# Sorting the attention's keys with a network of maxima and minima in a four-layer graph kernel

## The chip, the cores and the metric

The kernel runs on one core of one Trainium2 chip. The metric is the device time of one execution in microseconds. The kernel before took 3454.11 us in the median of three runs (3450.97 to 3459.17).

## The reference, cut to what matters

Four layers follow one another, each with a layer norm ahead of it and its result added to x, which has 6250 nodes of 256 values:

1. A graph layer: every one of 106250 edges joins its source's row with an edge attribute of 256 values, goes through a matrix W1 and a relu, and is averaged over its destination node.
2. A mixture of four experts, whose gates come from a graph attention over 131072 other edges.
3. A graph layer with a weight for each edge.
4. A second mixture of experts.

The change concerns the attention of layer 2. Its sum is a softmax over the edges of a destination:

```
e = leaky_relu(a_src[src] + a_dst[dst]);  e_max = segment_max(e, dst)
ee = exp(e - e_max[dst]);  denom = segment_sum(ee, dst)
agg = segment_sum(h[src] * ee / (denom[dst] + 1e-16), dst)
```

Its edges come in no order. Sums over a destination do not depend on the order either, so the kernel is free to sort.

## The kernel before, in words

The engines are TensorE (PE, matmuls), VectorE (DVE), ScalarE (ACT), GpSimd (POOL) and SyncE (SP). All arithmetic of the layers is in fp32. Nodes lie in 49 windows of 128, one node a partition.

The kernel first norms x and multiplies it with one half of W1 (y_dram). In this part `make_keys` builds, for every partition, 1024 keys of the attention's edges: one fp32 bit pattern each, with the destination (counted from the top) in its high bits and the source in its low ones. A larger key is a smaller destination, so that keys sorted downwards are edges sorted by destination.

Then comes the loop of the first graph layer (from L1598), which the change lives in. It has 147 iterations q and two more to drain: three for each window w, with six tiles of 128 edges in each. In iteration q,

- `join(q - 1)` (VectorE, L1485) adds the gathered source rows to the product of the edge attributes, and ScalarE does the relu (L1486);
- `hidden(q, 0)`, `hidden(q, 2)` and `hidden(q, 4)` (TensorE) multiply the transposed attributes `et` with the other half of W1 into `ph`, two tiles at a time;
- `add_up(q - 2)` (TensorE, L1508, L1500 for the last window) sums the rows of each destination, by a matmul with the 0/1 matrix `eq`;
- `load_sources(q + 2)` (GpSimd, L1128) gathers six source rows for each partition, and `load_attr` (SyncE, L1376) loads edge attributes up to four iterations ahead;
- `turn(q + 1)` (VectorE, L1467) transposes the attributes of the next iteration in blocks of 32 x 32 into `et`;
- `equal(q)` (VectorE, L1217) writes `eq`. A window's edges are sorted by destination already, so a tile needs only some quarters of its 128 nodes (`QUARTERS`); the last window takes all four.

Three generators fill the gaps between these: `work` (the end of each window, `end_of`, L1514), `sort` (the attention's sort) and `slow` (`windows`, which finds the edges of later windows, and ends near iteration 80). `steps` lets each of its generators do one step. `end_of`, `windows` and `sorted_edges` share a single PSUM buffer named pt.

The loop's order is fixed: `ordered.pin()` chains the instructions of each engine in the order in which the program gives them. So on VectorE and on TensorE an instruction that waits holds up all that stands behind it. The order in the loop around the change:

```
if 0 < q <= NQ1: join(q - 1)
if q < NQ1: hidden(q, 0)
steps(sort)
... add_up(q - 2); load_sources(q + 2); turn(q + 1); load_attr
if q < NQ1: hidden(q, 2)
steps(*([sort] if q % 2 else []))
... equals[q] = equal(wk, *groups1[q]); hidden(q, 4)
steps(slow)
```

The sort before (`sort_steps`, L1276) takes the eight largest keys of a partition with one instruction (L1279), writes them to `order`, and strikes them out of `key` with another (L1282, two instructions on the engine). 106 rounds give the 848 largest. Each of the two is one step; there is one step in each iteration between `join` and `turn` and, in odd iterations, a second one ahead of `equal`. The sort so takes 212 steps and is done in iteration 141. Then `sorted_edges` (L1285) runs as one piece: it takes the sources and the two halves of the destination out of `order`, turns one of these with five matmuls and sends it to DRAM (`low_dram`), and fills and compares limits with 160 small memsets.

The second part, the experts of layer 2 and their attention, begins when the loop has drained at about 1310 us; layers 3 and 4 follow. The change touches none of these.

Of the kernel before, what the change touches and what calls it, by code (L numbers as in the profile page):

```python
# [8 lines left out]
F32 = mybir.dt.float32  # L9
I32 = mybir.dt.int32  # L10
AF = mybir.ActivationFunctionType
OP = mybir.AluOpType
# [4 lines left out]
P = 128  # L17
# [851 lines left out]
def kernel(ctx: ExitStack, tc: tile.TileContext, a: dict, out: bass.AP):  # L869
# [11 lines left out]
    T = -(-N // P)  # L881
# [10 lines left out]
    C2 = E2 // P  # L892
# [6 lines left out]
    G1 = 6  # L899
    NG = CW // G1  # L900
    NT = G1 // 2
    NR = CW // NT
    Q = P // 4
    QUARTERS = ((0, 1), (0, 2), (1, 3), (1, 4), (2, 4), (3, 4))
# [16 lines left out]
    KA, KB, KT, KM, NK = 640, 544, 848, 596.0, 12  # L921
# [5 lines left out]
    V, SC, TE, GP, SY = nc.vector, nc.scalar, nc.tensor, nc.gpsimd, nc.sync  # L927
# [4 lines left out]
    def near_blocks(g):  # L932

        k = g * G + G / 2
        mid = k * (N / KM) / P
        spread_of = (C2 * (k / C2) * (1 - k / C2)) ** 0.5 * (N / KM) / P
        n = min(NK, int(-(-2 * (4.2 * spread_of + 0.9) // 1)))
        b0 = min(max(round(mid - n / 2), 0), T - 2)
        return b0, min(max(round(mid - n / 2) + n, b0 + 2), T) - b0
# [4 lines left out]
    with ExitStack() as fast:  # L944
# [51 lines left out]
        if T1 > C1:  # L996
            V.memset(flat.bitcast(I32)[:, C1:T1], 2**24)
            n = E1 - C1 * P
# [199 lines left out]
        def quarters(w, k):  # L1198

            return QUARTERS[k] if w < T - 1 else (0, 4)  # L1200

        def chunk(q):


            return [(k, t) for k in (q, q + NG) for t in range(NT)]

        def equal(pool, w, q):


            eq = pool.tile([P, G1 * P], F32, name="eq", bufs=3)  # L1210
            found, at = {}, 0
            for k in (q, q + NG):
                lo, hi = quarters(w, k)
                n = (hi - lo) * Q
                found[k] = eq[:, at : at + NT * n].rearrange("p (t n) -> p t n", n=n)
                at += NT * n
                V.tensor_tensor(  # L1217
                    found[k], lane[:, None, lo * Q : hi * Q].to_broadcast([P, NT, n]),
                    dst1[:, w, k, :].unsqueeze(2).to_broadcast([P, NT, n]), op=OP.is_equal,
                )  # L1220
            return found
# [51 lines left out]
            )  # L1273
            V.tensor_tensor(key.bitcast(I32)[:, half], raw[0], raw[1], op=OP.bitwise_or)

        def sort_steps(k):  # L1276

            top = order[:, k * 8 : (k + 1) * 8]
            V.max(out=top, in_=key)  # L1279
            yield  # L1280
            if k * 8 + 8 < KT:
                V.match_replace(out=key, in_to_replace=top, in_values=key, imm_value=0.0)  # L1282
            yield

        def sorted_edges(pst, wk):  # L1285

            k = order.bitcast(I32)
            V.tensor_scalar(src2, k[:, 0:KA], 8191, None, op0=OP.bitwise_and)
            some = key[:, 0:KT]
            for v, s in ((high, 20), (low, 13)):  # L1290
                vi = some.bitcast(I32)
                V.tensor_scalar(
                    vi, k, s, 127, op0=OP.logical_shift_right, op1=OP.bitwise_and
                )
                V.tensor_copy(some, vi)
                V.tensor_scalar(some, some, -1.0, 127.0, op0=OP.mult, op1=OP.add)
                V.tensor_copy(v, some)
            for c in range(KA // P):
                pt = pst.tile([P, 4, P], F32, name="pt")
                TE.transpose(pt[:, 0, :], some[:, c * P : (c + 1) * P], ident)  # L1300
                lt = wk.tile([P, P], BF16, name="lt")
                SC.activation(lt, pt[:, 0, :], AF.Copy)
                SC.dma_start(low_dram[c * P : (c + 1) * P, :], lt)
            V.tensor_add(good2[:, 1:2], good3[:, 0, 0:1], good3[:, 1, 0:1])
            V.tensor_add(good2[:, 3:4], good3[:, 0, 1:2], good3[:, 1, 1:2])

            lim = key[:, 0:KA]
            for g in range(KA // G):
                V.memset(lim[:, g * G : (g + 1) * G], float(near_blocks(g)[0]))
            hit = order[:, 0:KA]  # L1310
            V.tensor_tensor(hit, high[:, 0:KA], lim, op=OP.is_ge)
            for g in range(KA // G):
                V.memset(lim[:, g * G : (g + 1) * G], sum(near_blocks(g)) - 0.5)
            V.tensor_tensor(lim, lim, high[:, 0:KA], op=OP.is_ge)
            V.tensor_mul(hit, hit, lim)
            V.tensor_reduce(good2[:, 0:1], hit, axis=AX.X, op=OP.add)
# [5 lines left out]
        with ExitStack() as layer:  # L1322
            layer.enter_context(counting)
            srt = layer.enter_context(tc.tile_pool(name="srt", bufs=1))
            key = srt.tile([P, C2], F32, name="key")
            order = srt.tile([P, KT], F32, name="order")
            wp = layer.enter_context(tc.tile_pool(name="w1", bufs=1))
            wix = layer.enter_context(tc.tile_pool(name="wix", bufs=1))
            wea = layer.enter_context(tc.tile_pool(name="ea1", bufs=3, side="right"))
# [55 lines left out]
            with (  # L1385
# [12 lines left out]
                for t0, t1 in parts0:  # L1398
                    b = t0 // TB
# [5 lines left out]
                    for i in range(t1 - t0):  # L1405
                        t = t0 + i
# [29 lines left out]
            with (  # L1436
# [21 lines left out]
                def load_sources(q):  # L1458

                    w, g = groups1[q]  # L1460
                    for j, (k, t) in enumerate(chunk(g)):
                        gather(rows_of(q)[:, j, 0:D], y_dram, src1[:, w, k, t : t + 1])
# [9 lines left out]
                def hidden(q, j):  # L1472
                    if j == 0:
                        ph[q] = psh.tile([P, G1, D], F32, name="ph")
                    for i in range(j, j + 2):
                        mm(
                            ph[q][:, i, :],
                            lambda c: et[q][:, c, i * 4 : (i + 1) * 4, :].rearrange("p m k -> p (m k)"),
                            lambda c: w1b[:, c, :],
                        )  # L1480

                def join(q):

                    h = rows_of(q)[:, :, 0:D]
                    V.tensor_add(h, ph.pop(q), h)  # L1485
                    SC.activation(h, h, AF.Relu)  # L1486
                    et.pop(q)
# [79 lines left out]
                def windows():  # L1567

                    for b in range(1, NB):
                        for w in range(b * TB, (b + 1) * TB):  # L1570
                            count_below(w)
                            yield
                        find_starts(psm, b)
                        yield
                        yield from load_windows(b, psm)
                        if b == 1:
                            count_good()
                            yield

                def sorting():  # L1580

                    for k in range(KT // 8):
                        yield from sort_steps(k)
                    sorted_edges(psm, wk)

                work, sort, slow = [], [sorting()], [windows()]

                def steps(*more):
                    for some in (*more, work):
                        for n in list(some):  # L1590
                            if next(n, some) is some:
                                some.remove(n)
# [5 lines left out]
                for q in range(NQ1 + 2):  # L1598
                    if 0 < q <= NQ1:
                        join(q - 1)  # L1600
                    if q < NQ1:
                        hidden(q, 0)
                    steps(sort)
                    if q >= 2:
                        add_up(q - 2)
                        if (q - 2) % NG == NG - 1:
                            work.append(end_of((q - 2) // NG))
                    if 3 <= q + 2 < NQ1:
                        load_sources(q + 2)
                    if q + 1 < NQ1:  # L1610
                        turn(q + 1)
                        for n in range(q + 2, min(q + 5, NQ1)):
                            if n not in ahead:
                                ahead[n] = load_attr(n)
                    if q < NQ1:
                        hidden(q, 2)
                    steps(*([sort] if q % 2 else []))
                    if q < NQ1:
                        equals[q] = equal(wk, *groups1[q])
                        hidden(q, 4)  # L1620
                    steps(slow)
                    ordered.pin()
# [113 lines left out]
        with (  # L1736
# [404 lines left out]
            steps, begun, waiting = [[edge_columns(), False]], [], []  # L2141
# [43 lines left out]
            for k in range(NA + 5):  # L2185
# [4 lines left out]
                now, here, there, before = k - 2, k - 3, k - 4, k - 5  # L2190
# [30 lines left out]
            k = NA + 5  # L2221
# [14 lines left out]
        with (  # L2236
# [297 lines left out]
            k = 0  # L2534
# [21 lines left out]
        with (  # L2556
# [6 lines left out]
            n = wk.tile([P, NB + 7], F32, name="n")  # L2563
# [4 lines left out]
            for i in range(2):  # L2568
                k = NB + 1 + 2 * i
# [6 lines left out]
            some = wk.tile([P, 1], F32, name="some")  # L2576
# [48 lines left out]
```

## Time and profile before

| | us |
|---|---|
| Median of three runs | 3454.11 (3450.97 to 3459.17) |
| The profiled execution, its own time | 3456.93 |
| Its span, from first to last instruction | 3455.0 |
| PE busy in the span | 3184.3 (92%) |
| DVE busy | 2305.0 (67%) |
| POOL busy | 2240.7 (65%) |
| ACT busy | 1132.5 (33%) |
| First step of the sort, last step of the sort | 89.8, 1234.1 |

The profile shows one execution. A group of instructions is named by its line in the kernel, its engine, its operation and the tiles it writes and reads, with how often it ran, its busy time in all and the mean of one. Behind it stands the idle time of the engine just ahead of these instructions, and what ended it. Busy times of TensorE have modelled ends, so a busy TensorE is not one at its peak. What counts is which engine sets the pace in a stage, and what it waits for there.

### The profile page before, as it was taken

What the parts mean: (1) busy time and instruction counts of PE and PEld (TensorE: products, weight loads), DVE (VectorE), ACT (ScalarE), POOL (GpSimd) and SP (SyncE); (2) the same over time, 40 slices, a digit from 0 to 9 for tenths busy, and PEclk for the clock granted to TensorE, in tenths of its full rate; (3) what the DMA queues carried; (4) which work ended last, traced back from release to release, by engine and by line L of the source; (5) the groups of instructions that cost most, each with busy time, mean ns of one, the idle gap of its engine ahead of it and who ended that gap; (6) DMA issues with size and microseconds to landing.
All of it is one profiled execution on the core that took longest, in us unless ns stands there. A gap on an engine that the chain in (4) does not pass through costs nothing.

```text
span 3455.0 us, 56503 instructions
## 1 busy us (share of the span) xinstructions
PE 3184.3 (92%) x18509; PEld 2532.5 (73%) x18509; DVE 2305.0 (67%) x5687; ACT 1132.5 (33%) x2014; POOL 2240.7 (65%) x2364
## 2 busy tenths in 40 slices
PE   7899998999999999999999999995678888989898
PEld 5677776777777768888888888893456666666677
DVE  7788888888887876887576757775334444445464
ACT  4122222222222224344545454662012212112133
POOL 0577776777777754766555556634777777777773
PEclk8999999999999999999999999996567777677797
DMA  5899999999999963434334434443112222222221
GB/s 171 200 202 200 196 189 185 192 204 196 209 201 205 200 161 93 109 84 118 101 100 113 117 100 122 118 85 104 52 53 59 59 60 59 59 59 61 64 63 37
DMA packets 699194, 428.51 MB, mean 124 GB/s; under 512 B 531304, under 2 KB 640347, under 8 KB 698892
## 3 DMA queue, kind: packets, MB, share of 16 engines
q1 hardware_dynamic: 601436, 245.05, 30.0%
q0 software_dynamic: 89408, 178.08, 23.0%
q8 instruction: 150, 2.46, 0.3%
q10 hardware_dynamic: 8048, 1.68, 0.2%
q14 instruction: 152, 1.25, 0.1%
HBM read 382.05 MB, written 42.49 MB: 123 GB/s over the span
## 4 chain that ended last, share of the span: by engine, by line
PE 45%; DMA 14%; POOL 13%; DVE 12%; issue 9%; SPq 5%; ACT 2%; DVEq 0%; ACTq 0%; POOLq 0%
PE ph L1115 19%; POOL hg L1128 12%; PE py L1115 11%; PE po L1850 5%; DMA hg<-hp_dram,src 5%; DMA ea<-in_edge_attr_dram 5%; SPq L1376 4%; DVE et L1467 3%; PE pe L2490 2%; PE pt L1115 2%; DVE h L1485 2%; PE pe L1508 2%; DMA rb<-low_dram 2%; DVE order L1279 1%; PE pa L1787 1%
## 5 line engine op out<-in xcount | busy, mean ns | idle before, releaser
L1128 POOL DMA_INDIRECT h<-y_dram,src x882 | 837.0, 949 | 450.5 <-issue 331.8
L1128 POOL DMA_INDIRECT hg<-hp_dram,src x831 | 786.5, 946 | 268.0 <-issue 224.6
L1115 PE MATMUL ph<-w1b,et 128*128 128x256 f32 x3528 | 840.7, 388 | 21.1 <-DVE et L1467 19.7
L1128 POOL DMA_INDIRECT sg<-gat_dram,src x640 | 612.2, 957 | 355.9 <-issue 161.0
L1115 PEld LDWEIGHTS ph<-w1b,et 128*128 128x128 f32 x3528 | 656.1, 192 | 170.9 <-issue 67.7
L2490 PE MATMUL pe<-eq,hg 128*128 128x96 f32 (+15 forms) x2036 | 436.3, 352 | 151.4 <-DMA hg<-hp_dram,src 123.6
L2490 PEld LDWEIGHTS pe<-eq,hg 128*128 128x128 f32 x2036 | 384.7, 258 | 256.2 <-issue 96.7
L2469 DVE TENSOR_SCALAR eq<-px,dst,ew 128x96 f32<-128x96 f32 x831 | 261.9, 369 | 218.7 <-PE pe L2490 135.1
L1115 PE MATMUL py<-w,hh 128*128 128x256 f32 x1568 | 385.6, 386 | 6.0 <-ACT hh L1686 5.4
L1115 PE MATMUL ph<-b_all,w 128*128 128x256 f32 (+1 forms) x1600 | 385.8, 380 | 1.3 <-issue 1.2
L1486 ACT ACTIVATE h<-h 128x1536 f32<-128x1536 f32 x147 | 218.2, 1485 | 399.5 <-DVE h L1485 348.8
L1115 PEld LDWEIGHTS py<-w,hh 128*128 128x128 f32 x1568 | 290.0, 191 | 42.7 <-ACT hh L1686 8.0
L1115 PEld LDWEIGHTS ph<-b_all,w 128*128 128x128 f32 x1600 | 289.9, 190 | 33.8 <-issue 1.6
L1485 DVE TENSOR_TENSOR h<-ph,h 128x1536 f32<-128x1536 f32 x147 | 258.0, 1755 | 42.0 <-PE ph L1115 24.4
L1467 DVE STREAM_TRANSPOSE et<-ea 128x1536 f32<-128x1536 f32 x147 | 259.9, 1768 | 12.3 <-DMA ea<-in_edge_attr_dram 8.0
L1686 ACT ACTIVATE hh<-ph,b 128x256 f32<-128x256 f32 (+1 forms) x400 | 166.6, 467 | 282.0 <-PE ph L1115 277.1
L1850 PE MATMUL po<-pp,B 128*128 128x240 f32 (+10 forms) x1280 | 252.2, 337 | 3.0 <-DVE acc L1856 2.9
L1850 PEld LDWEIGHTS po<-pp,B 128*128 128x128 f32 x1280 | 215.6, 190 | 15.3 <-DVE acc L1856 3.8
L1508 PE MATMUL pe<-h,eq 128*32 128x257 f32 x3168 | 216.8, 384 | 0.0
L1508 PEld LDWEIGHTS pe<-h,eq 128*32 128x32 f32 x3168 | 96.0, 109 | 91.8 <-issue 33.8
L1829 DVE TENSOR_TENSOR pp<-px,A 128x960 f32<-128x960 f32 (+10 forms) x160 | 156.0, 975 | 3.9 <-PE po L1850 3.6
L1110 ACT ACTIVATE b_all<-pt 128x256 f32<-128x256 f32 x147 | 55.0, 383 | 275.3 <-PE pt L1109 274.8
(338 smaller groups left out, 4026.6 us busy)
## 6 DMA issues: line engine op xcount, KB each, us to landing
ea<-in_edge_attr_dram SPq DMA_DIRECT2D x1176, 96.0 KB
y<-y SPq DMA_DIRECT2D x196, 128.0 KB
w<-in_L_ffn_W_dram SPq DMA_DIRECT2D x48, 512.0 KB
y<-ys SPq DMA_DIRECT2D x96, 256.0 KB
rb<-low_dram SPq DMA_DIRECT2D x80, 256.0 KB
h<-y_dram,src POOLq DMA_INDIRECT x882
hg<-hp_dram,src POOLq DMA_INDIRECT x831
sg<-gat_dram,src POOLq DMA_INDIRECT x640
```

The lines of the kernel that those rows point to most:

```text
L1115: TE.matmul(dst, lhs(c), rhs(c), start=c == 0, stop=c == n - 1)
L1128: GP.indirect_dma_start(out=dst, out_offset=None, in_=table[0:NP, :], in_offset=IndirectOffsetOnAxis(ap=idx, axis=0),)
L1376: SY.dma_start(ea[c * Q : (c + 1) * Q, i, :, :], part[:, 2 * c * Q : 2 * (c + 1) * Q].rearrange("(m p) d -> p m d", p=Q),)
L1467: V.transpose(et[q].rearrange("p c m k -> p m c k"), ahead.pop(q).rearrange("p i m (c k) -> p (i m) c k", c=2),)
L1485: V.tensor_add(h, ph.pop(q), h)
L1486: SC.activation(h, h, AF.Relu)
L1508: TE.matmul(sums[w][b * Q : (b + 1) * Q, :], eq[k][:, j, at], h[:, i * NT + j, 0:WS], start=g == 0 and j == NT - 1, stop=g == last_of[b] a ...
L1686: SC.activation(hidden[u][:, f, :n, :], ph[:, f - f0, :n, :], AF.Gelu, bias=b1[:, e, f : f + 1],)
L1829: V.tensor_tensor(pps[g, half][:, :, 0:n, :], pay[:, js, :].unsqueeze(2).to_broadcast([P, HG, n, HV]), near[g][:, js, 0:n].unsqueeze(3).to ...
L1850: TE.matmul(po.rearrange("p b v -> p (b v)"), B[:, j, :], pp[:, j, 0:n, :].rearrange("p b v -> p (b v)"), start=half == 0 and j == 0, stop ...
L2469: V.tensor_scalar(equals[k][:, j, :], lanes[:, 0:NW], dst_of[:, t : t + 1], ew[:, t : t + 1], op0=OP.is_equal, op1=OP.mult,)
L2490: TE.matmul(sums[b][:, lo - t0 * P : hi - t0 * P], hg[:, j, :], eq[:, j, lo - n0 : hi - n0], start=False, stop=after >= (t0 + n) * P,)
```

## The change

The sort becomes a bitonic network. It goes through the sizes 2, 4, ... 1024, and in each size through the steps size/2, ... 1. In each of the 55 passes every key is compared with the one `step` away, the larger goes to one place and the smaller to the other, by one instruction for the maxima and one for the minima, from one of two buffers into the other. Up to size 512 neighbouring runs are sorted in opposite directions, so that a pass has two such pairs of instructions with 256 elements each; in the last size it has one pair with 512. A pair is one step of the generator. After 55 passes, an odd number, the keys lie in `order`.

Both buffers hold 1024 keys now, so `order` grows from 848 to 1024. `equal` gives room: its tile has the size that the largest iteration of an ordinary window needs, half of what it had, and the last window has a tile of its own, `eq4`, with one buffer. The second slot for a step of the sort, in odd iterations, is gone.

```diff
+        EQ = NT * Q * max(
+            sum(QUARTERS[k][1] - QUARTERS[k][0] for k in (q, q + NG)) for q in range(NG)
+        )
+
         def equal(pool, w, q):
-            eq = pool.tile([P, G1 * P], F32, name="eq", bufs=3)
+            total = NT * Q * sum(hi - lo for lo, hi in (quarters(w, q), quarters(w, q + NG)))
+            if w < T - 1:
+                eq = pool.tile([P, EQ], F32, name="eq", bufs=3)
+            else:
+                eq = pool.tile([P, total], F32, name="eq4", bufs=1)
...
-        def sort_steps(k):
-
-            top = order[:, k * 8 : (k + 1) * 8]
-            V.max(out=top, in_=key)
-            yield
-            if k * 8 + 8 < KT:
-                V.match_replace(out=key, in_to_replace=top, in_values=key, imm_value=0.0)
-            yield
+        def sort_steps():
+
+            here, there = key, order
+            size = 2
+            while size <= C2:
+                step = size // 2
+                while step:
+                    a, b = (
+                        v.rearrange("p (n m t s) -> p n m t s", m=size // (2 * step), t=2, s=step)
+                        for v in (here, there)
+                    )
+                    runs = [(slice(0, None, 2), 0), (slice(1, None, 2), 1)]
+                    for some, up in runs if size < C2 else [(slice(0, 1), 0)]:
+                        x, y = a[:, some, :, 0, :], a[:, some, :, 1, :]
+                        V.tensor_tensor(b[:, some, :, up, :], x, y, op=OP.max)
+                        V.tensor_tensor(b[:, some, :, 1 - up, :], x, y, op=OP.min)
+                        yield
+                    here, there = there, here
+                    step //= 2
+                size *= 2
+            assert here is order
 
         def sorted_edges(pst, wk):
-            k = order.bitcast(I32)
+            k = order.bitcast(I32)[:, 0:KT]
...
-            order = srt.tile([P, KT], F32, name="order")
+            order = srt.tile([P, C2], F32, name="order")
...
                 def sorting():
-                    for k in range(KT // 8):
-                        yield from sort_steps(k)
+                    yield from sort_steps()
                     sorted_edges(psm, wk)
...
-                    steps(*([sort] if q % 2 else []))
+                    steps()
```

## The prediction

> **What bounds the kernel now.** I read the page first, then the granted clock (0.90 on the one core), the groups by shape, the windows by stage, the waits, and the timeline around single waits. The sort lies wholly in the first graph layer, the loop from 117 to about 1310 us. Busy times in it:
>
> ```profile
> core 0: us, PE busy (x) PEld busy (x) DVE busy (x) ACT busy (x) POOL busy (x), PEclk, DMA share, GB/s
> 130.00:800.00 670.00, 642.05 (x4229) 490.69 (x4228) 575.62 (x941) 180.73 (x294) 473.11 (x500) 0.99 0.95 197
> 800.00:1225.00 425.00, 419.60 (x2776) 322.06 (x2775) 343.55 (x503) 120.94 (x199) 307.44 (x325) 1.00 1.03 202
> ```
>
> TensorE (PE) is busy for 95.8% of the first stretch and 98.7% of the second, VectorE (DVE) for 86% and 81%. So TensorE sets this stage, and only its idle time, 28.0 + 5.4 us, is there to be won: whatever leaves VectorE. What is the idle time waiting for? The waits from 120 to 800 us (engine and line, released by, total us, times, longest):
>
> ```profile
> PE ph L1115 <- DVE et L1467: 9.4, 21, 2.5
> PE pt L1109 <- DVE ix_g L1164: 8.3, 1, 8.3
> PE pt L1109 <- DVE dst L1170: 4.5, 3, 2.3
> PE pt L1109 <- DVE start L1036: 3.0, 2, 2.1
> PE pt L1115 <- DVE ix_g L1164: 2.1, 3, 0.7
> ```
>
> Nearly all is "VectorE came late": with the transposed edge attributes (et), or with emptying the one PSUM tile pt that the windows' small matmuls and end_of share. From 800 on only et is left (5.1 us, 18 times, in the waits from 800 to 1220). How a late et comes about, in every third iteration, the timeline shows (start, length, instruction, idle before):
>
> ```profile
> 911.17 0.42 DVE L1532 TENSOR_TENSOR o<-pt,b 128x256 f32<-128x256 f32 x1 [3.78 <-PE pt L1115]
> ...
> 913.05 1.76 DVE L1485 TENSOR_TENSOR h<-ph,h 128x1536 f32<-128x1536 f32 x1
> ...
> 914.72 1.22 DVE L1279 MAX8 order<-key 128x8 f32<-128x1024 f32 x1
> ...
> 916.41 1.78 DVE L1467 STREAM_TRANSPOSE et<-ea 128x1536 f32<-128x1536 f32 x1 [0.21 <-issue]
> ...
> 918.33 0.89 PE L1115 MATMUL ph<-w1b,et 128*128 128x256 f32 x3 [0.23 <-DVE et L1467]
> ```
>
> VectorE had been idle for 3.78 us, so it starts this chain on time; the sort's step sits between join (L1485) and turn (L1467), and TensorE waits 0.23 us at the end. The durations:
>
> ```profile
> L1279 DVE MAX8 order<-key 128x8 f32<-128x1024 f32 x106 | 127.9, 1207 | 0.0
> L1282 DVE MATCH_REPLACE8 key<-order,key 128x1024 f32<-128x1024 f32 x105 | 126.8, 1208 | 0.0
> L1282 DVE MATCH_VALUE_LOAD key<-order,key 128x8 f32 x105 | 7.5, 71 | 0.0
> L1532 DVE TENSOR_TENSOR o<-pt,b 128x256 f32<-128x256 f32 x49 | 20.8, 424 | 126.3 <-PE pt L1115 126.3
> L1263 DVE TENSOR_TENSOR last<-last,ix_g 128x512 f32<-128x512 f32 x2 | 1.4, 688 | 0.0
> L1264 DVE TENSOR_REDUCE good<-last 128x1 f32<-128x512 f32 x2 | 1.4, 676 | 0.0
> L1809 DVE TENSOR_REDUCE z<-za 128x32 f32<-128x384 f32 x37 | 31.2, 843 | 0.3
> ```
>
> [...] L1809 reads fp32 at a step of 16 bytes: against L1264, 384 elements take 1.7 cycles each in place of one[...]. [...] The gathers that overlap L1217[...] last 954 ns in the mean against 946 for the rest: next to nothing.
>
> **The change, part by part.**
>
> *Removed:* 127.9 + 126.8 + 7.5 = 262.2 us of VectorE.
>
> *Added:* the sizes 2 to 512 make 45 passes with four instructions of 256 elements, the last ten passes two of 512: [...] Net 172 us less, 5% of the span, but not on TensorE. The step is unknown in the trace for two strided SBUF inputs. Lower bound one cycle per element (L1888 reads runs of four fp32 at that pace: 196 elements in 356 ns); upper bound 1.7 from L1809. [...] I take one cycle; at 1.7 throughout a pair is 1.22 us.
>
> *In an iteration:* the first slot (between join and turn) held one step of 1.21 to 1.29 us; it gets a pair, 2 x 0.424 + gap = 0.88 us: 0.35 us earlier. In q = 90 to 99 the pair is 1.4 us, 0.15 later. The second slot, every odd iteration, between turn and equal, is emptied: 1.25 us earlier for equal, the windows' step and the next join. The network has 100 yields against 212, so it ends at q = 100 and not at 141; the 46 iterations after have no sort.
>
> *Waits for et:* in the windows 1 to 29, about 21 regular ones of 0.27 go, and some 2 us of the longer: 7.5 us. In q = 90 to 99 nothing is won (-0.6). After q = 100, 14 of 0.29: 4. Together 11 us.
>
> *Waits for pt:* 13 stalls, 19.8 us. What VectorE is nearer to the evacuation: 1.6 us in odd iterations, 0.35 in even. The stall of 8.3 us follows a wait of 9.6 us for a transfer (raw_src) and loses 1.6 at most. About half the stalls are each kind: 7 us.
>
> *sorted_edges moves* from q = 141 behind turn to q = 100 ahead of turn. It is 15.8 us of VectorE (L1288 at 1247.1 to L1316 at 1262.9), and TensorE, in order, waits 5.7 us for the first of its five transposes and then for each copy. Behind it stand add_up and the rest of the iteration on TensorE, turn and join on VectorE. Before, the two windows from there took 59.1 us join to join against 2 x 23.55: 12 us lost. In the new place TensorE has hidden(q,0) out of the way, resumes after some 9.7 us, has add_up and hidden(q,2), (q,4) to do (5.2 us), and turn(q+1) lands 17.8 us after the block's start: 12 to 15 us. I count 0, the end is 3 worse. Its five stores go out on the Activation queue as before.
>
> *eq and eq4:* the smaller eq costs nothing in time. eq4 has one buffer: equal(145) waits for add_up(144) (1296.25 at its end, where equal(145) ran at 1287.9), and join(145) behind it comes at 1297.4 in place of 1291.7; add_up(145) at 1301.3 is still met. equal(146) then ends at 1305.2, join(146) at 1307 in place of 1303.4, and add_up(146) is 2.5 to 3.5 us later. The first expert layer's matmuls can fill that; where they don't, 3.5 us. I take 2.
>
> *GpSimd, DMA:* a window of three iterations issues 18 gathers at 1.25 us = 22.5 us against TensorE's 23.3 with its idle taken out; slices of 220 GB/s and more stand beside the mean of 202. Both still cover, with little to spare.
>
> Sum: 11 + 7 - 0 - 2 = 16 us. The profiled execution took 3456.9 us (span 3455.0 and 1.9 around it): 3441. It lies 2.8 above the median of the runs, 3454.1, which becomes 3438. The stages after it run on TensorE too (busy 199 of 200 us from 1400), so the gain is kept.
>
> **Rivals.**
>
> *Nothing to measure.* The gaps close, and something with as little slack takes their place: gathers at 22.5 of 23.3, or edge attributes. For: shares of DMA near 1. Against: both are off the chain at present, gathers being issued 15 us before their join. 3454 less 0 to 6: 3451.
>
> *Much faster.* The ends of matmuls are modelled, so "busy" can hide waits for VectorE. For: its busy 81 to 86%. Against: its idle time shows it waiting for TensorE 58 us at L1532 from 800 to 1225. With a hidden 0.3 us in each of 147 iterations: -44, 3410.
>
> *Slower: strided operands.* If an element of the network's passes costs more than the 1.7 cycles of L1809, the first slot grows and et comes later in each of the 33 windows under the sort. The gains outside that slot are some 7 us net (4 after q = 100, 5 at pt, less 2); they are eaten at 0.21 us more per window, a pair of 1.46 us, 2.15 cycles per element. At 3 cycles a pair is 1.9 us, 33 x 0.66 = 22 lost, net +15: 3469. [...]
>
> **How the numbers follow.** My forecast (8 to 28 us faster) 0.60; much faster 0.10; nothing 0.16; slower 0.14, of it 0.03 for sorted_edges and the last window at their dear ends. A measurement of this kernel can tell about 0.2% (7 us) from no change. The range leaves out half of much faster and most of slower: 3421 to 3457. The forecast alone: 3426 to 3446. Faster 0.70, same 0.16, slower 0.14.
>
> **What would show it.** [...] the waits of PE for et from 130 to 1225 down from 16 us to under 5; waits at pt roughly halved; sorted_edges near 930 us in place of 1247, with a stall of 10 us; equal of the last window waiting for PE pe L1500. The prediction is wrong if the pairs take over 1.4 us, if TensorE's idle time moves to gathers or ea, or if the loop's period falls well below 23.3 us a window.

## The result, and the profile after

The changed kernel took 3430.09 us in the median of six runs (3423.36 to 3434.85) beside 3455.03 us of the kernel before: a ratio of 0.9927, 95% interval 0.9914 to 0.9941, so 25 us or 0.7% faster. The forecast was 3438. The profiled execution of after took 3423.36 us (span 3421.6), the fastest of its six, so a difference of the two profiles (33.4 us of span) is some 8 us larger than one of medians.

Busy times of the loop's two stretches in the kernel after (columns as in the windows of before):

```profile
core 0: us, PE busy (x) PEld busy (x) DVE busy (x) ACT busy (x) POOL busy (x), PEclk, DMA share, GB/s
130.00:800.00 670.00, 658.36 (x4377) 507.70 (x4376) 509.82 (x953) 184.28 (x307) 497.16 (x519) 1.00 1.01 204
800.00:1215.00 415.00, 407.18 (x2690) 313.63 (x2689) 266.98 (x564) 114.49 (x198) 300.39 (x315) 0.99 1.00 201
```

In the first stretch TensorE's idle time went from 28.0 to 11.6 us; in the second it is 7.8 us, 6.6 of them in the one window with `sorted_edges`. VectorE's share fell from 86 to 76% and from 81 to 64%. What TensorE still waits for from 120 to 800 us:

```profile
PE pt L1109 <- DVE ix_g L1164: 3.4, 1, 3.4
PE pt L1115 <- DVE ix_g L1164: 2.1, 3, 0.7
...
PE pt L1109 <- DVE dst L1170: 1.8, 3, 0.6
...
PE ph L1115 <- DVE et L1489: 0.8, 1, 0.8
```

The wait for et is down from 21 times, 9.4 us, to a single one, and those for pt are about half (10.7 us in all against 19.8). In the third iteration of a window, where before the late et cost a visible 0.23 us, the timeline of after reads:

```profile
1009.65 0.42 DVE L1554 TENSOR_TENSOR o<-pt,b 128x256 f32<-128x256 f32 x1 [4.98 <-PE pt L1115]
...
1011.52 1.76 DVE L1507 TENSOR_TENSOR h<-ph,h 128x1536 f32<-128x1536 f32 x1
...
1013.76 1.78 DVE L1489 STREAM_TRANSPOSE et<-ea 128x1536 f32<-128x1536 f32 x1 [0.21 <-DMA ea<-in_edge_attr_dram]
...
1016.20 0.38 PE L1109 MATMUL pt<-ident,o 128*128 128x128 f32 x2
...
1016.41 1.89 PE L1115 MATMUL ph<-w1b,et 128*128 128x256 f32 x8
```

VectorE is idle longer ahead of the chain (4.98 us against 3.78), no sort step stands between join (L1507) and turn (L1489), et is ready at 1015.5, and TensorE passes from the transposes to `ph` with no wait shown.

The groups by shape of the network, and of the last window's `eq4`:

```profile
L1300 DVE TENSOR_TENSOR order<-key 128x256 f32<-128x256 f32 x46 | 19.9, 433 | 0.0
...
L1300 DVE TENSOR_TENSOR key<-order 128x512 f32<-128x512 f32 x5 | 3.4, 689 | 0.0
...
L1225 DVE TENSOR_TENSOR eq<-lane,dst 128x384 f32<-128x384 f32 x6 | 3.0, 547 | 14.7 <-PE pe L1522 14.7
```

All eight groups of maxima and minima lie at 418 to 433 ns for 256 elements and at 682 to 689 for 512; they sum to 90.1 us, as forecast.

Where the time went, by the joins of the two profiles (us). Window w lies between join(3w) and join(3w + 3); the time between them is called its period below.

| stretch | before | after | difference |
|---|---|---|---|
| start to the first join | 117.3 | 114.2 | -3.1 |
| window 0 | 21.6 | 20.8 | -0.7 |
| windows 1 to 29 | 709.1 | 684.4 | -24.7 |
| windows 30 to 47 | 436.2 | 427.4 | -8.8 |
| last window: joins 144 to 146 | 19.1 | 24.0 | +4.9 |
| join 146 to the end of the span | 2151.6 | 2150.7 | -0.9 |

Nearly all of the change acts in three of these rows: 24.7 + 8.8 - 4.9 = 28.6 us. The rest of the kernel keeps what was won; between two profiles of the same changed kernel this rest varied by more than the 0.9 us in the table (2150.7 and 2157.1 from join 146 on).

### The profile page after: what moved, and what is told of

Read it like the earlier page. It is cut to its first block, busy times and chain, and to the rows that moved or that the text cites. A ratio compares the mean times of both kernels' runs of the same rounds, so it can differ in the third digit from the quotient of the medians.

```text
span 3421.6 us, 56392 instructions
## 1 busy us (share of the span) xinstructions
PE 3172.9 (93%) x18509; PEld 2532.1 (74%) x18509; DVE 2137.7 (62%) x5571; ACT 1123.3 (33%) x2014; POOL 2247.8 (66%) x2364
## 4 chain that ended last, share of the span: by engine, by line
PE 61%; POOL 15%; DMA 9%; issue 8%; DVE 4%; ACT 2%; SPq 1%; DVEq 0%; ACTq 0%; POOLq 0%
PE ph L1115 30%; POOL hg L1128 13%; PE py L1115 11%; PE po L1871 6%; PE pe L1530 5%; DMA hg<-hp_dram,src 5%; PE pt L1115 4%; PE pe L2511 2%; POOL h L1128 1%; PE pa L1808 1%; SPq L1398 1%; DMA rb<-low_dram 1%; PE pt L1109 1%; DMA ea<-in_edge_attr_dram 1%; DMA h<-y_dram,src 1%
## 5 line engine op out<-in xcount | busy, mean ns | idle before, releaser
L1507 DVE TENSOR_TENSOR h<-ph,h 128x1536 f32<-128x1536 f32 x147 | 258.2, 1757 | 101.3 <-PE ph L1115 73.8
L1489 DVE STREAM_TRANSPOSE et<-ea 128x1536 f32<-128x1536 f32 x147 | 260.5, 1773 | 12.0 <-DMA ea<-in_edge_attr_dram 8.1
```

Source lines behind the costliest of these rows:

```text
L1489: V.transpose(et[q].rearrange("p c m k -> p m c k"), ahead.pop(q).rearrange("p i m (c k) -> p (i m) c k", c=2),)
```

## Experiments

Two theories stood against each other at first. *Place:* what counts is when turn comes after join, so the sort step between them is to blame, and the rest of the gain is pt coming free earlier. *Load:* VectorE simply had 172 us too much, wherever that stood. Later ones ask what is left. Kernels that ran in different groups ran on different chips (before: 3454.98 in the first, 3462.19 in the second, 3457.02 in the third), so only ratios are compared across groups. "Loop" below is the time from join(3) to join(144) in the profile: 1145.5 us before, 1111.9 after, 1113.8 in a second profile of after.

**Only the place (b_moved).** The kernel before with its old sort, the same instructions on VectorE, but no step between join and turn:

```diff
                         hidden(q, 0)
-                    steps(sort)
+                    steps()
...
-                    steps(*([sort] if q % 2 else []))
+                    steps(*([sort, sort] if q % 2 else [sort]))
```

> The kernel before, with its old sort, but each iteration's step of the sort stands behind turn instead of between join and turn; odd iterations take their two steps there. VectorE's work is the same to the instruction. Theory A (it is the place: what stands between join and turn makes et late, and a wait of 0.27 us costs about 0.47 us a window): the waits of PE for et from 130 to 1225 fall from 16 us to under 4, the windows' period without the windows' own work falls from 23.55 to about 23.1 us, and the kernel takes 3440 us (3432 to 3446); stalls at pt do not get shorter. Rival B (it is the sum of VectorE's work, 172 us less): the same time as before, 3450 to 3459.

Measured: 3436.09 us, ratio 0.995 (0.9936 to 0.9964). Its loop takes 1121.0 us, 24.5 less than before, with not one instruction taken off VectorE. Its waits of TensorE from 120 to 800 us:

```profile
PE pt L1109 <- DVE ix_g L1164: 5.5, 1, 5.5
PE pt L1109 <- DVE dst L1170: 4.6, 3, 2.4
PE pt L1109 <- DVE start L1036: 3.2, 2, 2.2
PE ph L1115 <- DVE et L1467: 2.7, 3, 1.4
```

The waits for et fall from 21 to 3, while those for pt stay nearly as they were (18.1 us in all, against 19.8). So the place does most of it: 24.5 of the 33.6 us that the change takes off the loop. That the rest comes from the emptied second slot is tested below (a_slot2).

**The first slot filled again (a_slot1).** The changed kernel with idle maxima between join and turn, which bring the slot back to about the old step's length (`pad` is a new tile of 8 values; its line is left out here):

```diff
                         hidden(q, 0)
+                    if q < 90:
+                        V.max(out=pad, in_=flat[:, 0:200])
+                    elif 100 < q <= 141:
+                        V.max(out=pad, in_=flat)
+                        V.max(out=pad, in_=lane)
                     steps(sort)
```

> The kernel after, with idle maxima between join and turn that bring this slot back to about 1.25 us in iterations 0 to 89 and 101 to 141 (200 elements beside a pair of the network, 831 and 128 elements where there is no pair). The second slot stays empty. A: the waits for et come back, 44 windows at 0.47 us: 20 us on the 3430 of after, 3450 (3443 to 3455), and the period after iteration 101 is 23.5 us again. B: 84 of the 172 us of VectorE's work are back, so half of the gain: 3442, and the period in between.

Measured: 3446.24 us, 0.9975 (0.9967 to 0.9983); loop 1130.8, 18.9 more than after. The mean period of windows 35 to 46 is 23.69 us instead of 23.05 (23.65 in most of them), and the waits of TensorE from 930 to 1215 us hold one line:

```profile
PE ph L1115 <- DVE et L1490: 5.1, 12, 0.7
```

Twelve waits, 0.43 us in the mean as shown (0.36 in most); 0.64 us a window as the loop pays it. In windows 1 to 29 the same kernel loses 8.9 us, some 0.3 a window, though from 120 to 800 us the view shows a single wait for et. Window 27, for one, takes 23.39 us against 23.06 in after, with 0.10 us of idle time on TensorE. So a late et costs time that the view does not show; how much, is worked out below.

**The second slot filled again (a_slot2).** In odd iterations behind turn, up to q = 141, for the step that the change took away there:

```diff
                         hidden(q, 2)
+                    if q % 2 and q <= 141:
+                        V.max(out=pad, in_=flat)
+                        V.max(out=pad, in_=lane)
                     steps()
```

> The kernel after, with idle maxima of 1.27 us behind turn in odd iterations up to 141, where the old sort had its second step; the slot between join and turn stays short. A: only the stalls at the shared PSUM tile pt come back, which lie before iteration 80: 7 to 11 us, 3439 (3435 to 3444), and the period after iteration 101 stays at 23.05 us. B: 90 of 172 us are back: 3443, spread evenly, with a longer period after iteration 101 too.

Measured: 3435.74 us, 0.995 (0.9936 to 0.9963); loop 1119.5, 7.6 more than after. The period after iteration 101 stays at 23.05. Most of what it costs lies in windows 1 to 29 (6.1 us), where TensorE's idle time goes from 11.1 to 18.1 us. Of these 7.0 us, 4.8 are shown at pt and 2.4 at ph, behind VectorE's work on a window's end (rc).

**Both (a_both).**

> The kernel after with both slots filled as in the two kernels above: VectorE's timetable is that of before, the network and the place of sorted_edges are new. A: 3430 + 20 + 9 = 3459 (3453 to 3464), that is before plus the 4.8 us by which the last window with one eq4 buffer is later. If moving sorted_edges were part of the gain, it would stay: 3445 or less.

Measured: 3454.79 us, 1.0001 (0.9993 to 1.0009); loop 1143.3. With VectorE's two slots at their old length the whole gain is gone, although the sort is a network and `sorted_edges` still stands at iteration 100. The two halves add up: 0.0048 + 0.0023 of the ratio alone, 0.0074 together (in the loops of the profiles 18.9 + 7.6 us alone, 31.4 together, 5 us more). Moving `sorted_edges` is worth nothing that can be seen: in its new place its window takes 35.78 us, 12.1 more than the mean of its neighbours (23.65), and in the old place it cost 12.0.

**No sort at all (a_nosort).** One copy takes the network's place:

```diff
-                    yield from sort_steps()
+                    V.tensor_copy(order, key)
+                    for _ in range(100):
+                        yield
...
```

> The kernel after without the network: one copy takes its place, the keys stay unsorted, 100 empty steps keep sorted_edges at iteration 100; the comparison at the end that would start the general path is set never to be true. It leaves out the sort, so the attention is not the reference's. Theory A (only the slot's length ahead of turn counts, and a pair of 256 elements is short enough): only the four windows of the last ten passes gain, 2 us: 3428 (3422 to 3432). Rival B (VectorE's sum counts, 25 us for 172): 90 us less give 13 us: 3417.

Measured: 3424.91 us, 0.9894 (0.9879 to 0.9909). Its loop takes 1112.5 us, as after's 1111.9 and 1113.8. In the loop as a whole, then, the 90 us of network that are left cost nothing that can be seen. Windows 29 to 32, where a pair of the network has 512 elements, do run at 23.05 us in place of 23.60, 2.2 us in all as expected, but the window of `sorted_edges` is 1.2 us longer here (35.12). The ratio, however, lies 0.0033 below after's and the intervals do not meet: where before takes 3455 us it is 3418, rival B's figure and not A's. After was not run on this chip; two kernels that ran both here and on the last group's chip (a_eq4, a_best) had ratios lower by 0.0007 and 0.0002 here, which is the smaller part of it. The profile, of the slowest of the four runs, does not put the difference in the loop, where B would have it; where it lies stays open.

**The last window with two tiles of the ordinary kind (a_eq4, eq4_again).**

```diff
...
-                eq = pool.tile([P, EQ], F32, name="eq", bufs=3)
-            else:
-                eq = pool.tile([P, total], F32, name="eq4", bufs=1)
...
+            parts = [(q, q + NG)] if w < T - 1 else [(q,), (q + NG,)]
...
+            for ks in parts:
+                eq, at = pool.tile([P, EQ], F32, name="eq", bufs=4), 0
...
```

> The kernel after, but the last window's 0/1 matrices lie in two ordinary eq tiles each, four buffers of 384 elements in all (less memory than now), so equal(145) and equal(146) wait for no earlier add_up. If the single eq4 buffer costs what the traces show at the end of the loop (4.8 us between the last but two join and the last): 3425 (3420 to 3428), with the idle 4.7 us of TensorE near the loop's end gone. If the expert layer's matmuls fill that time anyway: 3430.

> a_eq4 again, beside the changed kernel on one chip. If the single buffer of the last window's matrices costs the 4.9 us that the trace shows, the ratio to the kernel before lies 0.0014 below that of the changed kernel beside it; if the end of the layer hides it, the two ratios are equal.

Measured: 3425.83 us, 0.9902 (0.9887 to 0.9917), and again 3426.92, 0.9909 (0.9895 to 0.9923). In both profiles joins 144 to 146 take 19.1 us as before the change, against 24.0. The comparison of the last window waits 2.4 us in place of 14.7 (groups by shape of eq4_again):

```profile
L1223 DVE TENSOR_TENSOR eq<-lane,dst 128x384 f32<-128x384 f32 x6 | 3.1, 552 | 2.4 <-PE pe L1520 2.4
```

Beside the changed kernel on one chip the ratio is 0.0018 lower, where 0.0014 was expected; the intervals overlap, so the 4.9 us are shown by the trace and only made likely by the times.

**`sorted_edges` spread over some 28 iterations (a_spread).** One instruction or so a step, in place of one block:

```diff
-        sorted_edges(psm, wk)
+        yield from sorted_edges(psm, wk)
...
             for c in range(KA // P):
...
                 SC.dma_start(low_dram[c * P : (c + 1) * P, :], lt)
+                yield
...
```

> The kernel after with sorted_edges cut into some 28 steps of at most 0.65 us of VectorE, one an iteration from 100 on, instead of one block of 15 us. If the block's cost is TensorE's wait of 5 us, four small ones, and the clock and order behind them (10.9 us more in that window than in its neighbours): 3420 (3416 to 3424), and that window has a period of 23.1. If VectorE's steps only make et late in 28 iterations instead: 3426 or more.

Measured: 3430.98 us, 0.9909 (0.9896 to 0.9923). The block's own window is down from 33.96 to 22.91 us, but windows 36 and 37 take 25.21 and 28.20, so that only some 3.7 of the 11 us stay (the ratio is 3424 us where before takes 3455, the dear end of what was expected). In these the trace of VectorE, TensorE and the queues shows

```profile
969.94 0.34 ACTq L1330 DMA_DIRECT2D low_dram<-lt  x1
...
977.45 0.34 ACTq L1330 DMA_DIRECT2D low_dram<-lt  x1
...
977.48 0.44 PE L1109 MATMUL pt<-ident,o 128*128 128x128 f32 x2 [1.69 <-ACT lt L1329]
...
979.42 1.78 DVE L1503 STREAM_TRANSPOSE et<-ea 128x1536 f32<-128x1536 f32 x1 [3.68 <-DMA ea<-in_edge_attr_dram]
```

Turn waits for edge attributes that come late, four times and 10.6 us in all near there. My first reading was that at a period of 23.05 us their transfers are the next bound. The next experiment was made against it.

**The same without transposes and stores (a_nolow).** The edit against a_spread; the zeros are stored once, ahead of the sort.

```diff
             for c in range(KA // P):
-                pt = pst.tile([P, 4, P], F32, name="pt")
-                TE.transpose(pt[:, 0, :], some[:, c * P : (c + 1) * P], ident)
-                lt = wk.tile([P, P], BF16, name="lt")
-                SC.activation(lt, pt[:, 0, :], AF.Copy)
-                SC.dma_start(low_dram[c * P : (c + 1) * P, :], lt)
                 yield
...
```

> a_spread with the transposes of the block on the sorted edges, their evictions on ScalarE and their stores left out of the loop (the DRAM copy that they fill is filled with zeros at the start, so the low bits of the sorted edges are left out of the computation); VectorE's part of the block stays spread over the iterations. Theory E (at a period of 23.05 us without a pause the loads of the edge attributes are the next bound, and the block's pause had let them catch up): the waits for the edge attributes near windows 36 and 37 of the spread kernel, 10.6 us in 4 waits, stay at 6 to 11 us, and the time is about that of a_spread, 3424 to 3431. Theory S (the seven stores or the transposes of the spread block hold these loads or the turn up): the waits are under 2 us, windows 36 and 37 take 23.0 to 23.2 us each, and the loop from the third to the 144th join takes 7 to 8 us less than in a_spread (1109.3 there, so about 1102).

Measured: 3419.62 us, 0.9896 (0.9881 to 0.9911); loop 1101.2 against 1109.3 in a_spread, 8.1 less. (The block has five such stores, not the seven of the expectation.) The windows view of the second stretch:

```profile
800.00:1215.00 415.00, 413.74 (x2763) 319.84 (x2763) 272.49 (x578) 116.68 (x197) 310.11 (x324) 1.00 1.03 206
```

TensorE is idle for 1.3 us of 415, windows 36 and 37 take 22.97 and 23.05, and no late edge attribute holds up turn by more than 0.2 us. So the transfers of edge attributes are not a bound at 23.05 us. What held them up in a_spread its SyncE queue tells, in the waits from 900 to 1030 us:

```profile
SPq L1412 <- DMA low_dram<-lt: 31.4, 5, 16.3
SPq L1412 <- DVE et L1503: 16.3, 5, 5.6
```

The issue of an edge-attribute load waits for a store of the sort, five times: after the store issued at 969.94 a load that was held for 16.3 us is issued at 972.11, and all loads behind it in SyncE's queue were held with it. In the changed kernel the block's five stores go out within 4.3 us (897.65 to 901.92) while the whole loop stands still; there too a load is held, 18.8 us at the longest, at no further cost. The records of that trace show what store and load have in common. The loads of the loop name eight semaphores for their end (100, 102 to 107 and 109), and the five stores name five of the same: 100, 102, 104, 105 and 107. The next loads on these five numbers are issued 1.5 to 2.1 us after the store on theirs, the first at 899.24 behind the store at 897.65. So in these traces one number serves two queues, and a load waits for a store. a_nolow leaves out the transposes and evictions together with the stores, so that the semaphore alone would mend it was not tried; one of TensorE's waits, the 1.69 us for `lt` above, belongs to the shared pt and would stay.

**Both repairs (a_best, best_again).** a_eq4 and a_spread together; and the changed kernel once more (after_again), with eq4_again and this one on one chip.

> The two edits above together. If they are independent: 3430 - 5 - 10 = 3415 (3409 to 3420). If one hides the other: 3420.

> The changed kernel unaltered, for a direct comparison on one chip with the two kernels run beside it: 0.9927 of the kernel before again, between 0.990 and 0.995.

> a_best again (two buffers for the last window's matrices and the block on the sorted edges spread), beside the changed kernel on one chip. By the loop and tail of the profiles, 3.7 + 4.9 = 8.6 us less than the changed kernel, a ratio 0.0025 lower; if the spread block only moves its loss, 4.9 us and 0.0014, as eq4_again.

Measured: a_best 3424.81 us, 0.9893 (0.9878 to 0.9908) (3418 us where before takes 3455, as expected); but its loop, 1112.9 us, is not shorter than after's (1111.9 and 1113.8). Then, side by side: after_again 3433.93 us, 0.9927 (0.9914 to 0.9941); eq4_again 0.9909; best_again 3419.99 us, 0.9895 (0.988 to 0.991). The last interval lies below that of the changed kernel: this version beats both kernels, by 14 us and by 37 us in the medians. In the profiles it wins 3.6 us in the loop and 4.9 in the last window on after_again, 8.5 as expected; another 5.0 lie after join 146, in code that none of these kernels alters, and are within what that part varies by. Against eq4_again the intervals overlap, so what the spread block adds by itself is not shown by the times.

## Why the prediction was right, and where it was not

The direction, the stage, the mechanism and the range held. The size was put too low, 16 us in place of 25: the gains at et and pt came out 12 us larger, and 3 us of that went by luck into a larger loss in the last window. By the steps:

- **The network's cost, 90.1 us.** Exact: it is 180 x 0.424 + 20 x 0.688 us, with the durations that L1532 and L1263 have before for 256 and 512 elements. By these two an element takes (688 - 424) / 256 = 1.03 ns, which stands for the prediction's cycle, and an instruction 160 ns besides; L1809's 843 ns for 384 elements at a step of 16 bytes make 1.78 ns an element, the 1.7 cycles. This bound was about right as well, in the one pass that reads and writes at that step throughout, size 2: its four instructions took 623, 612, 684 and 646 ns (596 to 630 in after_again), where 160 + 256 x 1.7 x 1.03 make 608 by this estimate; the next pass is back at 0.42 us. In the timeline of after:

```profile
115.88 0.68 DVE L1299 TENSOR_TENSOR order<-key 128x256 f32<-128x256 f32 x1
...
121.86 0.42 DVE L1299 TENSOR_TENSOR key<-order 128x256 f32<-128x256 f32 x1
```

  Why this step is slow, no run shows. The slower rival, strided operands, was excluded by this: only four instructions of 200 come near 1.7 cycles.

- **Waits for et, 11 us: right in kind, half the size.** This is the term of the sum that failed. I multiplied waits that the view shows (21 and 14) by the idle time that it shows (0.27 us). The loop's period, 23.55 us in the mean of two neighbouring windows without a stall at pt, fell to 23.05: 0.5 us in 28 windows up to 28 and in 14 from 34 on, 21 us. The traces show where the missing part was. In the timeline of before, at the place of the late et:

```profile
917.72 0.38 PE L1109 MATMUL pt<-ident,o 128*128 128x128 f32 x2
...
918.33 1.97 PE L1115 MATMUL ph<-w1b,et 128*128 128x256 f32 x8 [0.23 <-DVE et L1467]
```

  The first matmul for ph starts 0.61 us after the transposes of pt; in the timeline of after, shown above, 0.21. That is 0.40 us for a wait shown as 0.23: where nothing waits, the next matmul starts 0.17 us before the end that the record gives the transposes (1016.20 + 0.38), and a wait is shown from that end on. The eight matmuls that follow took 1.97 us before and 1.89 after. Together that is 0.48, the 0.5 us of the period. Other windows agree: beside the 23.05 us of a window without a wait, the period grows by TensorE's idle time and some 0.24 us more. Idle times of 0.10 (a_slot1, window 27), 0.27 (before, the mean), 0.31 (after, windows 29 to 32) and 0.36 us (a_slot1, most windows from 35 on) go with 0.33, 0.50, 0.55 and 0.60 us. And each window before, up to 46, had at least 0.23 us of idle time, while the view lists 21 such waits in 29 windows. (The waits for et that the two views of before list make 9.4 + 5.1 = 14.5 us and not the 16 of the prediction's signs; after, they are 2.0.) The profile's ends of matmuls are modelled, with which the overlap of 0.17 us in the records agrees; what the missing time consists of, no run isolates. b_moved agrees on the price: 23.55 to 23.05 with the waits gone.

- **The rival "much faster"** had the right cause, time hidden in TensorE's busy, and the wrong count: it is hidden about once a window, where a wait stands, and not in each of 147 iterations. By the 0.24 us above, in 42 windows, it is some 10 us of the 44 it claimed.

- **Windows 29 to 32 (q = 90 to 99), nothing won.** Right: with a pair of 512 elements their period is 23.60, with a wait of 0.31 us shown in each; before the change it was 23.55.

- **Waits for pt, 7 us.** They went from 19.8 to 10.7 us as shown, 9.1. The 8.3 us stall after the late raw_src lost 4.9, not the 1.6 that I gave it "at most". In part the transfer was less late: VectorE waited 9.6 us for raw_src before and 6.7 after. From the instruction that had waited to TensorE's start it took 10.3 us before and 7.9 after. The stall is 3.6 us in a_slot1, 5.0 in a_slot2, 5.5 in b_moved and 7.4 in a_both; why raw_src came earlier is not shown.

- **sorted_edges, 0.** It cost 12.0 us over its two windows before and 10.9 in one after, 1 us won where I had none. TensorE waits for the first transpose and then for each copy, as worked out:

```profile
PE pt L1322 <- DVE key L1318: 4.9, 1, 4.9
PE pt L1322 <- ACT lt L1324: 1.6, 4, 0.5
```

  It began at 891.9 us and not near 930: I had read its place off the old loop's clock without taking off what the windows ahead of it would gain.

- **The last window, 2 us, at most 3.5.** It lost 4.9. The waits are the forecast ones, in the timeline of after:

```profile
1258.93 1.03 DVE L1225 TENSOR_TENSOR eq<-lane,dst 128x384 f32<-128x384 f32 x2 [8.27 <-PE pe L1522]
...
1268.10 1.03 DVE L1225 TENSOR_TENSOR eq<-lane,dst 128x384 f32<-128x384 f32 x2 [6.47 <-PE pe L1522]
```

  Reckoned from join 144, join 145 was forecast at 13.1 us and came at 13.0. The step that failed is "add_up(145) at 1301.3 is still met": that is 17.0 after join 144, and it began at 18.4. All behind it came 1.3 to 1.4 us later than forecast, join 146 at 24.0 in place of 22.7, add_up(146) at 28.3, 4.9 later than before where I had 2.5 to 3.5. And the first expert layer's matmuls, which I let fill part of it, filled none that can be seen: from join 146 to the end takes 2153.2 us in the mean of the eight profiles that lost the 4.9 us, and 2153.1 in the mean of the six that did not. Two tiles give the 4.9 back (a_eq4).

- **The rival "nothing to measure"** failed: a gather takes 958 ns in place of 949, and with the block's stall gone as well (a_nolow) TensorE runs with 1.3 us of idle time in 415. At 23.05 us a window this loop is at TensorE's own pace, below the 23.3 that I had taken for it out of the busy times; that the period might fall below it I had named as a sign against me, and it did, by 0.25.

Summed: 21 + 9 + 1 - 5 = 26 us by these readings, 25 in the medians, 16 in the forecast.

## What to carry to other kernels

When one engine whose order is fixed feeds another, look at what stands between the operand's last reader and its next writer before counting busy time: moving the same instructions out of that one slot (b_moved) won three quarters of what replacing them won in the loop (24.5 of 33.6 us). Price a TensorE wait by the period of the loop with and without it, not by the idle time that the waits view shows; here a regular wait for et cost some 0.24 us more than it showed. And where a block is cut into small steps, follow its DMAs: in a_spread a load on SyncE's queue waited for up to 16.3 us for a store of the block on another queue.

## What the runs showed of the hardware that was not expected

- A regular wait of TensorE for et costs the loop's period some 0.24 us more than the idle time that the profile shows: 0.33 us for 0.10, 0.50 for 0.27, 0.55 for 0.31, 0.60 for 0.36.
- A store of 32 KB on the Activation queue held a load on SyncE's queue for up to 16.3 us (a_spread); in the trace of after the five stores and the loads name the same semaphores. Two windows of a_spread are 2.2 and 5.2 us longer; without the stores and their transposes (a_nolow) they are not.
- fp32 maxima and minima at a step of 16 bytes took 612 to 684 ns for 256 elements (596 to 630 in a second profile); in the later passes of that size they took mostly 0.42 us.
